# Four 32-column tiles against one full product in a bias MLP, and folded weight products in the self-attention after it

## The chip, the cores and the metric

The kernel runs on one core of one Trainium2 chip. The metric is device time in microseconds of one execution. The profile is one execution taken by the hardware profiler; its times are in microseconds from the first instruction.

## What is computed

Two layers follow each other on an input x of 2 x 512 x 32 x 32, all in fp32.

The first is a deformable attention block with 8 groups of 64 channels. Its costly part is a small network that gives a bias to every pair of a query position (1024) and a sampled key position (64), in each of 16 groups (2 images, 8 heads). Cut to what matters:

```python
pos = grid_q[:, :, None, :] - grid_kv[:, None, :, :]        # 16 x 1024 x 64 x 2
bias = jnp.sign(pos) * jnp.log1p(jnp.abs(pos))
bias = jax.nn.relu(bias @ cpb_w1 + cpb_b1)                  # 2 -> 128
bias = jax.nn.relu(bias @ cpb_w2 + cpb_b2)                  # 128 -> 128
bias = (bias @ cpb_w3 + cpb_b3)                             # 128 -> 1
attn = jax.nn.softmax(qh @ kh^T + bias, axis=-1)
out = attn @ vh
x = x + out_w out + out_b
x = x + mlp_w2 gelu(mlp_w1 bn(x) + mlp_b1) + mlp_b2         # 512 -> 2048 -> 512
```

The second is a plain self-attention over the 1024 positions of each image, with 512 channels:

```python
q, k, v = Wq x + bq, Wk x + bk, Wv x + bv
attn = softmax(q^T k / sqrt(512))
out = x + Wp (attn v) + bp
```

## The kernel before

The program is written in Tile, which places the waits and allots the buffers, and may move instructions of one engine past each other where no dependence forbids it. Four stages follow each other.

**Head.** q of all groups, the sampling offsets, the sampled keys and values. The key positions' features (`fea`) are written to a DRAM tensor `fdr` and read back in chunks, broadcast to all partitions (`st_tables`, L286).

**Bias loop.** 16 groups, each of 64 keys by 1024 queries. The x half of the first bias layer depends on the key and the query's column alone, the y half on the key and the query's row alone, so ScalarE makes a table `ta` (L292) and GpSimd a table `tb` (L295) for a chunk of 16 keys. `st_layer1` then forms one key's 128 channels x 1024 queries with one custom VectorE instruction that adds the two tables and clamps at zero (L306, tile `h1`, 6 buffers).

`st_layer2` takes a pair of keys. The 128 output channels are cut into two halves z. For each z a PSUM tile `ps2` gets 64 channels of the first key in partitions 0 to 63 and the same 64 channels of the second key in partitions 64 to 127, from four column tiles of 32 columns (L327), for each half h of the queries. ScalarE applies Relu with the bias (L333 for z = 0, `rx`) and, for z = 1, with a scale that is the third layer's weight taken positive (L336, `ry`). `st_pair` then lets VectorE add both halves, weighted, in one instruction (L342): the result still needs a sum over 64 partitions only, with signs.

`st_layer3` takes two pairs, 4 keys: one matmul of 32 columns for each pair and query half, into four column tiles of the group's score tile `sim` (L366). The weights are a window of the tile `w3s`, which is zero except in two columns, so the sums of one call land in the right rows. For the first two of a group's 16 calls (`DIRECT`) VectorE makes no sum and both halves go through matmuls. At a group's first call the product of q and k starts the accumulation (L353).

After a group's last call `softmax_steps` runs in four parts, one per loop turn: bias, transposes `pt` (L380), maximum, exponential, sum and scaling; transposes `pb` (L395); then for each half of the queries the product with the values `pa` (L402) and its copy. The loop runs over pairs; layer one is written two pairs ahead of layer two:

```python
if p + 2 < 2 * NS:
    st_layer1(p + 2)
if p < 2 * NS:
    st_layer2(p)
if 1 <= p <= 2 * NS:
    st_pair(p - 1)
if p % 2 == 1 and p >= 3:
    st_layer3(p // 2 - 1)
```

**MLP.** Output projection `pso` (L452), first product `psh` (L468), second product `psm` (L476), all full 128x128x512 matmuls; VectorE adds the residual into `xs` (L480).

**Self-attention.** The four weights are loaded into `wl_s`. For each image: q and k by `psp` (L505) with their biases on ScalarE (L509); the transposed values by `psv` (L514) with bv added on VectorE (L518); scores `pss` for 8 blocks of 128 queries (L525), softmax, transposes `psx` (L544); attention times values `psa` (L567), copied to `os_` (L571); the output projection `psf` (L575), bias and residual (L580), and the store.

Of the kernel before, what the change touches and what calls it, by code (L numbers as in the profile page):

```python
# [20 lines left out]
NSL = 16  # L21
KT = 16
DIRECT = 2
# [10 lines left out]
    ("bq", 4), ("bk", 4), ("bp", 4), ("dwb", 1), ("cb1", 1), ("cb3", 1),  # L34
    ("w1x", 1), ("w1y", 1), ("cb2a", 1), ("cb2b", 1), ("w3a", 1), ("w3b", 1), ("dww", 36),
# [10 lines left out]
def conv_seq_kernel(ctx: ExitStack, tc: tile.TileContext, x, kst, cst, vec, wsm, outw, w1, w2, wl, bv, out):  # L46
# [25 lines left out]


    sc = cp.tile([P, 4], F32, name="sc")
    nc.vector.tensor_scalar(sc[:, 0:1], col("w3b"), 0.0, 2.0, ALU.is_ge, ALU.mult)
    nc.vector.tensor_scalar(sc[:, 0:1], sc[:, 0:1], 1.0, None, ALU.subtract)
    nc.vector.tensor_tensor(sc[:, 1:2], sc[:, 0:1], col("w3b"), ALU.mult)
    nc.vector.tensor_tensor(sc[:, 2:3], sc[:, 0:1], col("w3a"), ALU.mult)
    nc.vector.tensor_tensor(sc[:, 3:4], sc[:, 1:2], col("cb2b"), ALU.mult)
    w3s = cp.tile([P, 62], F32, name="w3s")  # L80
    w3d = cp.tile([P, 62], F32, name="w3d")
    for t, src in ((w3s, sc[:, 0:1]), (w3d, col("w3a"))):
        nc.gpsimd.memset(t, 0.0)
        for u in range(2):
            nc.gpsimd.tensor_copy(t[64 * u : 64 * u + 64, 30 + u : 31 + u], src[64 * u : 64 * u + 64, :])

    dp = ctx.enter_context(tc.tile_pool(name="dp", bufs=1, space=bass.MemoryType.DRAM))
    fdr = dp.tile([NG, 4, 2 * W, KT], F32, name="fdr")
# [13 lines left out]
    with tc.tile_pool(name="ph", bufs=1) as ph, tc.tile_pool(name="ph2", bufs=2) as ph2, tc.tile_pool(  # L102
# [105 lines left out]
        for e in range(2):  # L208
            nc.vector.tensor_copy(
                kv.rearrange("p k b (e i t) -> p (k b) e i t", e=2, t=2)[:, :, e],  # L210
                pk.rearrange("p (g i e t) -> p g i e t", i=NSL, e=2, t=2)[:, :, :, e],
            )
# [45 lines left out]
        for c in range(4):  # L258
            nc.sync.dma_start(
                out=fdr[:, c, :, :].rearrange("g p j -> p g j"),  # L260
                in_=fea[0:64].rearrange("p f g (c j) -> p (f g) c j", c=4)[:, :, c, :],
            )
# [11 lines left out]
    with tc.tile_pool(name="lp", bufs=2) as lp, tc.tile_pool(  # L274
# [4 lines left out]
        NS = NG * NSL  # L279
        tabs, h1s, rxs, us, sims = {}, {}, {}, {}, {}  # L280


        def st_tables(c):
            b, k, f = groups[c // 4]
            fb = lp.tile([P, 2, W, KT], F32, name="fb", bufs=1)
            nc.sync.dma_start(  # L286
                out=fb.rearrange("p a x j -> p (a x j)"),
                in_=fdr[f * 8 + b * NCH + k, c % 4].rearrange("p j -> (p j)").partition_broadcast(P),
            )
            ta = lp.tile([P, KT, W], F32, name="ta", bufs=2)  # L290
            tb = lp.tile([P, KT, H], F32, name="tb", bufs=2)
            nc.scalar.activation(  # L292
                ta.rearrange("p j x -> p x j"), fb[:, 0], AF.Identity, bias=col("cb1"), scale=col("w1x")
            )
            nc.gpsimd.tensor_scalar(  # L295
                tb.rearrange("p j y -> p y j"), fb[:, 1], col("w1y"), 0.0, ALU.mult, ALU.add
            )
            tabs[c] = (ta, tb)

        def st_layer1(pair):  # L300
            for t in range(2):
                key = 2 * pair + t
                ta, tb = tabs[key // KT]
                j = key % KT
                h1 = lp.tile([P, HW], F32, name="h1", bufs=6)
# [7 lines left out]
                h1s[pair, t] = h1  # L313

        def paired(pair):
            return pair // 2 % NSL >= DIRECT

        def st_layer2(pair):  # L320
            h1 = [h1s.pop((pair, t)) for t in range(2)]
            for z in range(2):
                ps = zp.tile([P, 2, 512], F32, name="ps2")
                for h in range(2):
                    for q in range(4):
                        c0 = 64 * z + 32 * (q % 2)
                        nc.tensor.matmul(  # L327
                            ps[32 * q : 32 * q + 32, h, :], cw2[:, c0 : c0 + 32],
                            h1[q // 2][:, h * 512 : (h + 1) * 512], start=True, stop=True,
                        )  # L330
                if z == 0:
                    rx = lp.tile([P, 2, 512], F32, name="rx", bufs=3)
                    nc.scalar.activation(rx, ps, AF.Relu, bias=col("cb2a"))  # L333
                else:
                    ry = lp.tile([P, 2, 512], F32, name="ry", bufs=5)
                    nc.scalar.activation(ry, ps, AF.Relu, bias=sc[:, 3:4], scale=sc[:, 1:2])  # L336
            rxs[pair], us[pair] = rx, ry

        def st_pair(pair):
            if paired(pair):  # L340
                rx, ry = rxs.pop(pair), us[pair]
                nc.vector.scalar_tensor_tensor(  # L342
                    ry.rearrange("p h n -> p (h n)"), rx.rearrange("p h n -> p (h n)"), sc[:, 2:3],
                    ry.rearrange("p h n -> p (h n)"), ALU.mult, ALU.add,
                )

        def st_layer3(s):
            gi, i = divmod(s, NSL)
            b, k, f = groups[gi]
            if i == 0:  # L350
# [8 lines left out]
            for direct in (True, False):  # L359
                if direct and paired(2 * s):  # L360
                    continue
                for h in range(2):
                    for e in range(2):
                        q = 64 * h + 32 * e
                        src = rxs.pop(2 * s + e) if direct and h == 1 else (rxs if direct else us)[2 * s + e]
                        nc.tensor.matmul(  # L366
                            sims[gi][q : q + 32, :], (w3d if direct else w3s)[:, 30 - 2 * i : 62 - 2 * i],
                            src[:, h, :], start=False, stop=(not direct and i == NSL - 1),
                        )
            for e in range(2):  # L370
                us.pop(2 * s + e)

        def softmax_steps(gi):
            b, k, f = groups[gi]
            sim = sims.pop(gi)
            ss = lp.tile([P, 512], F32, name="ss", bufs=1)
# [7 lines left out]
            ex = lp.tile([P, 8, J], F32, name="ex", bufs=1)  # L384
# [11 lines left out]
            at = lp.tile([P, 512], F32, name="at", bufs=1)  # L396
# [13 lines left out]
        st_tables(0)  # L410
        st_layer1(0)
        st_layer1(1)
        for p in range(2 * NS + 2):
            if p % 8 == 1 and p // 8 + 1 < 4 * NG:
                st_tables(p // 8 + 1)
            if p + 2 < 2 * NS:
                st_layer1(p + 2)
            if p < 2 * NS:
                st_layer2(p)
            if 1 <= p <= 2 * NS:  # L420
                st_pair(p - 1)
            if p % 2 == 1 and p >= 3:
                s = p // 2 - 1
                st_layer3(s)
                if s % NSL == NSL - 1:
                    tail = softmax_steps(s // NSL)
                    due = p
            if tail is not None and p >= due:
                tail = tail if next(tail, 0) is None else None
                due = p + 1  # L430
# [55 lines left out]
    bvb = cp.tile([P, C], F32, name="bvb")  # L486
    nc.gpsimd.dma_start(out=bvb, in_=bv.partition_broadcast(P))
# [5 lines left out]
    with tc.tile_pool(name="sp", bufs=1) as sp, tc.tile_pool(  # L493
        name="sps", bufs=2, space=PSUM
    ) as sps, tc.tile_pool(name="spm", bufs=4, space=PSUM) as spm:
        for b in range(B):
            qs = sp.tile([P, NCH, HW], F32, name="qs")
            ks = sp.tile([P, NCH, HW], F32, name="ks")
            for i, (dst, bn) in enumerate(((qs, "bq"), (ks, "bk"))):
                for o in range(NCH):  # L500
                    for h in range(2):
                        n = slice(h * 512, (h + 1) * 512)
                        ps = spm.tile([P, 512], F32, tag="ps", name="psp")
                        for k in range(NCH):
                            nc.tensor.matmul(  # L505
                                ps, wl_s[:, i, k, o * P : (o + 1) * P], xs[:, k, b, n],
                                start=(k == 0), stop=(k == NCH - 1),
                            )
                        nc.scalar.activation(dst[:, o, n], ps, AF.Identity, bias=col(bn, o))  # L509
            vt = sp.tile([P, 8, C], F32, name="vt")  # L510
            for m in range(8):
                ps = spm.tile([P, 512], F32, tag="ps", name="psv")
                for k in range(NCH):
                    nc.tensor.matmul(  # L514
                        ps, xs[:, k, b, m * P : (m + 1) * P], wl_s[:, 2, k, :],
                        start=(k == 0), stop=(k == NCH - 1),
                    )
                nc.vector.tensor_tensor(vt[:, m, :], ps, bvb, ALU.add)  # L518
            aT = sp.tile([P, 8, HW], F32, name="aT")

            def scores(t):
                ps = sps.tile([P, 2, 512], F32, name="pss")
                for h in range(2):
                    for k in range(NCH):
                        nc.tensor.matmul(  # L525
                            ps[:, h, :], qs[:, k, t * P : (t + 1) * P], ks[:, k, h * 512 : (h + 1) * 512],
# [33 lines left out]

            os_ = sp.tile([P, NCH, HW], F32, tag="qs", name="os_")
            for h in range(2):
                n = slice(h * 512, (h + 1) * 512)
                for o in range(NCH):
# [6 lines left out]
                    nc.scalar.copy(os_[:, o, n], ps)  # L571
                for o in range(NCH):
# [100 lines left out]
```

## Time and profile before

| | us |
|---|---|
| median of 3 runs | 3253.16 (3252.32 to 3254.32) |
| the profiled execution | 3253.16, its span 3251.4, granted clock 0.991 |
| head, to the first layer-two product | 166 |
| bias loop, 166 to 2286 | 2120, TensorE busy 2112.1, VectorE 1823.0, ScalarE 1279.7 |
| MLP, 2286 to 2783 | 497, TensorE busy 496.2 |
| self-attention, 2783 to the end | 468, TensorE busy 457.5 |

The profile names an instruction by its line, engine and the tiles it writes and reads. "PE" is TensorE's matmuls and "PEld" its weight loads, which can lie under matmuls. The durations of single matmul records overlap and their ends are modelled; the pace is read from start to start. An fp32 matmul of the program is two records. "128*32" after a matmul is the size of the array's tile, "128x512" the moving operand.

### The profile page before, as it was taken

Reading aid. Unit: us, or ns where it says so; the run is one execution under the profiler, and the core shown is the slowest. Engines: PE = TensorE matmul, PEld = TensorE weight load, DVE = VectorE, ACT = ScalarE, POOL = GpSimd, SP = SyncE. Lnnn points to the kernel's source line nnn. Section 1 sums busy time; section 2 is a strip of 40 time slices with the busy share of each in tenths; the row PEclk is TensorE's granted clock in tenths of the full one; section 3 lists DMA queues with packets and bytes.
Section 4 is the critical chain, followed back from the end, with each engine's and each line's share of the span. In section 5 each row is a group of like instructions: output and inputs, shape, how many; then the busy total and the mean of one; then the engine's idle time right before and its main releaser. Section 6 shows DMA issues by size and latency. Waiting matters only on the chain.

```text
span 3251.4 us, 48875 instructions
## 1 busy us (share of the span) xinstructions
PE 3180.6 (98%) x21756; PEld 1138.4 (35%) x21756; DVE 2000.6 (62%) x1865; ACT 1415.4 (44%) x1329; POOL 137.8 (4%) x79
## 2 busy tenths in 40 slices
PE   8599999999999999999999999999999999999999
PEld 2344323223223232232322322322444444444444
DVE  3588989889888898898988988988010010030030
ACT  1366666656556565565665655655101101110110
POOL 0010000000000000000000000000000000000000
PEclk9799999999999999999999999999999999999999
DMA  1100000000000000000000000000200010000000
GB/s 69 36 27 20 14 14 21 14 21 14 21 14 21 14 21 14 21 14 19 15 19 16 18 17 14 21 14 1 91 1 0 0 45 8 0 0 16 10 0 26
DMA packets 21106, 60.36 MB, mean 19 GB/s; under 512 B 5984, under 2 KB 6240, under 8 KB 19744
## 3 DMA queue, kind: packets, MB, share of 16 engines
q1 hardware_dynamic: 20240, 55.84, 4.8%
q8 instruction: 171, 2.80, 0.4%
q10 hardware_dynamic: 576, 1.14, 0.1%
q0 software_dynamic: 80, 0.26, 0.0%
q14 instruction: 39, 0.32, 0.0%
HBM read 52.78 MB, written 4.46 MB: 18 GB/s over the span
## 4 chain that ended last, share of the span: by engine, by line
PE 97%; DVE 1%; ACT 1%; DMA 1%; issue 0%; SPq 0%; ACTq 0%; DVEq 0%
PE ps L327 55%; PE sim L366 8%; PE psm L476 7%; PE psh L468 7%; PE psa L567 3%; PE psp L505 3%; PE pss L525 3%; PE pc L152 2%; PE pso L452 2%; PE psf L575 2%; PE psv L514 2%; PE pa L402 1%; PE sim L353 1%; PE psq L126 0%; PE pkv L201 0%; PE psx L544 0%
## 5 line engine op out<-in xcount | busy, mean ns | idle before, releaser
L327 PE MATMUL ps<-h,kp 128*32 128x512 f32 x16384 | 1834.3, 593 | 11.7 <-DVE h L306 11.7
L306 DVE CUSTOM_DVE_ANT_1 h<-ta,tb 128x1024 f32<-128x1024 f32 x1024 | 1245.1, 1254 | 288.7 <-PE ps L327 261.5
L327 PEld LDWEIGHTS ps<-h,kp 128*32 128x32 f32 x16384 | 557.7, 110 | 1221.8 <-issue 1171.5
L333 ACT ACTIVATE rx<-ps,vs 128x1024 f32<-128x1024 f32 x512 | 571.4, 1116 | 510.9 <-PE ps L327 474.7
L336 ACT ACTIVATE ry<-ps,sc 128x1024 f32<-128x1024 f32 x512 | 614.9, 1201 | 294.2 <-PE ps L327 292.7
L342 DVE SCALAR_TENSOR_TENSOR ry<-rx,sc,ry 128x1024 f32<-128x1024 f32 x448 | 571.8, 1276 | 6.3 <-ACT ry L336 6.3
L366 PE MATMUL sim<-ry,w3s 128*32 128x512 f32 x2048 | 276.3, 592 | 0.9 <-DVE ry L342 0.9
L480 DVE SCALAR_TENSOR_TENSOR xs<-psm,vs,xs 128x512 f32<-128x512 f32 x16 | 12.0, 751 | 425.1 <-PE psm L476 425.1
L295 POOL TENSOR_SCALAR tb<-fb,vs 128x512 f32<-128x512 f32 x64 | 134.6, 2103 | 2061.0 <-DVE h L306 1899.8
L476 PE MATMUL psm<-hm,w_s 128*128 128x512 f32 x512 | 220.4, 592 | 0.0
L472 ACT ACTIVATE hm<-psh,vs 128x512 f32<-128x512 f32 x64 | 44.0, 687 | 377.7 <-PE psh L468 377.7
L468 PE MATMUL psh<-xn,w1b 128*128 128x512 f32 x384 | 165.5, 592 | 0.0
L476 PEld LDWEIGHTS psm<-hm,w_s 128*128 128x128 f32 x512 | 97.3, 190 | 122.5 <-issue 122.5
L366 PEld LDWEIGHTS sim<-ry,w3s 128*32 128x32 f32 x2048 | 69.7, 110 | 152.0 <-issue 148.9
L567 PE MATMUL psa<-aT,vt 128*128 128x512 f32 x256 | 113.9, 607 | 0.0
L525 PE MATMUL pss<-ks,qs 128*128 128x512 f32 x256 | 112.2, 592 | 0.0
L505 PE MATMUL psp<-xs,wl_s 128*128 128x512 f32 x256 | 110.3, 592 | 0.8 <-DVE xs L480 0.8
L580 DVE SCALAR_TENSOR_TENSOR res<-psf,vs,xs 128x512 f32<-128x512 f32 x16 | 12.0, 752 | 156.0 <-PE psf L575 156.0
L518 DVE TENSOR_TENSOR vt<-psv,bvb 128x512 f32<-128x512 f32 x16 | 11.1, 691 | 154.7 <-PE psv L514 154.7
L468 PEld LDWEIGHTS psh<-xn,w1b 128*128 128x128 f32 x384 | 73.0, 190 | 91.8 <-issue 91.8
L292 ACT ACTIVATE ta<-fb,vs 128x512 f32<-128x512 f32 x64 | 84.1, 1315 | 42.5 <-DMA fb<-fdr 32.9
L535 ACT ACTIVATE ex<-pss,mx 128x1024 f32<-128x1024 f32 x16 | 17.8, 1114 | 124.6 <-DVE mx L532 124.6
(114 smaller groups left out, 1148.7 us busy)
## 6 DMA issues: line engine op xcount, KB each, us to landing
fb<-fdr SPq DMA_DIRECT2D x64, 512.0 KB, 3.6
xs<-in_x SPq DMA_DIRECT2D x8, 512.0 KB, 9.7
w_s<-in_w SPq DMA_DIRECT2D x4, 1024.0 KB, 13.6
wl_s<-in_wl SPq DMA_DIRECT2D x4, 1024.0 KB, 7.8
out<-res SPq DMA_DIRECT2D x16, 256.0 KB, 2.0
w1b<-in_w SPq DMA_DIRECT2D x3, 1024.0 KB, 7.2
ow_s<-in_outw SPq DMA_DIRECT2D x1, 1024.0 KB, 6.2
w1a<-in_w SPq DMA_DIRECT2D x1, 1024.0 KB, 8.5
```

The lines of the kernel that those rows point to most:

```text
L295: nc.gpsimd.tensor_scalar(tb.rearrange("p j y -> p y j"), fb[:, 1], col("w1y"), 0.0, ALU.mult, ALU.add)
L306: nc.vector._custom_dve(TENSOR_ADD_SAT, out=h1.rearrange("p (y x) -> p y x", x=W), in0=ta[:, j, :].unsqueeze(1).to_broadcast([P, H, W]), i ...
L327: nc.tensor.matmul(ps[32 * q : 32 * q + 32, h, :], cw2[:, c0 : c0 + 32], h1[q // 2][:, h * 512 : (h + 1) * 512], start=True, stop=True,)
L333: nc.scalar.activation(rx, ps, AF.Relu, bias=col("cb2a"))
L336: nc.scalar.activation(ry, ps, AF.Relu, bias=sc[:, 3:4], scale=sc[:, 1:2])
L342: nc.vector.scalar_tensor_tensor(ry.rearrange("p h n -> p (h n)"), rx.rearrange("p h n -> p (h n)"), sc[:, 2:3], ry.rearrange("p h n -> p ...
L366: nc.tensor.matmul(sims[gi][q : q + 32, :], (w3d if direct else w3s)[:, 30 - 2 * i : 62 - 2 * i], src[:, h, :], start=False, stop=(not dir ...
L468: nc.tensor.matmul(ps, w1i, xn2[:, k, :], start=(k == 0), stop=(k == NCH - 1),)
L476: nc.tensor.matmul(ps, w2_s[:, i, o * P : (o + 1) * P], hm[:, i, :], start=(i == 0), stop=(i == NF - 1),)
L505: nc.tensor.matmul(ps, wl_s[:, i, k, o * P : (o + 1) * P], xs[:, k, b, n], start=(k == 0), stop=(k == NCH - 1),)
L525: nc.tensor.matmul(ps[:, h, :], qs[:, k, t * P : (t + 1) * P], ks[:, k, h * 512 : (h + 1) * 512], start=(k == 0), stop=(k == NCH - 1),)
L567: nc.tensor.matmul(ps, vt[:, m, o * P : (o + 1) * P], aT[:, m, n], start=(m == 0), stop=(m == 7),)
```

## The change

The change has two parts and belongs to two stages. Constants, tables and layouts follow: the kernel has one table chunk of 32 keys where it had two of 16, the key order of a group is laid out anew, the third layer's weights stand in one column of `w3p`, and `bv` goes into the packed vectors.

*Bias loop.* Layer two is one full 128x128 product for a key and query half, with all 128 channels of one key in the 128 partitions. VectorE's sum and the direct case are gone. Layer three takes a step of 2 keys with 128 channels each, so 512 steps in all. The loop runs over steps; layer one is written one step ahead; layer three of two steps is written together, at every second step.

```diff
-        def st_layer1(pair):
-            for t in range(2):
-                key = 2 * pair + t
-                ta, tb = tabs[key // KT]
-                j = key % KT
-                h1 = lp.tile([P, HW], F32, name="h1", bufs=6)
+        def st_layer1(s):
+            ta, tb = tabs[s // 16]
+            for e in range(2):
+                j = 2 * (s % 16) + e
+                h1 = lp.tile([P, HW], F32, name="h1", bufs=4)
...
-        def st_layer2(pair):
-            h1 = [h1s.pop((pair, t)) for t in range(2)]
-            for z in range(2):
+        def st_layer2(s):
+            for e in range(2):
+                h1 = h1s.pop((s, e))
                 ps = zp.tile([P, 2, 512], F32, name="ps2")
                 for h in range(2):
-                    for q in range(4):
-                        c0 = 64 * z + 32 * (q % 2)
-                        nc.tensor.matmul(
-                            ps[32 * q : 32 * q + 32, h, :], cw2[:, c0 : c0 + 32],
-                            h1[q // 2][:, h * 512 : (h + 1) * 512], start=True, stop=True,
-                        )
-                if z == 0:
-                    rx = lp.tile([P, 2, 512], F32, name="rx", bufs=3)
-                    nc.scalar.activation(rx, ps, AF.Relu, bias=col("cb2a"))
-                else:
-                    ry = lp.tile([P, 2, 512], F32, name="ry", bufs=5)
-                    nc.scalar.activation(ry, ps, AF.Relu, bias=sc[:, 3:4], scale=sc[:, 1:2])
-            rxs[pair], us[pair] = rx, ry
-
-        def st_pair(pair):
-            if paired(pair):
-                rx, ry = rxs.pop(pair), us[pair]
-                nc.vector.scalar_tensor_tensor(
-                    ry.rearrange("p h n -> p (h n)"), rx.rearrange("p h n -> p (h n)"), sc[:, 2:3],
-                    ry.rearrange("p h n -> p (h n)"), ALU.mult, ALU.add,
-                )
+                    nc.tensor.matmul(
+                        ps[:, h, :], cw2, h1[:, h * 512 : (h + 1) * 512], start=True, stop=True
+                    )
+                h2 = lp.tile([P, 2, 512], F32, name="h2", bufs=6)
+                nc.scalar.activation(h2, ps, AF.Relu, bias=col("cb2"))
+                h2s[s, e] = h2
...
-            for direct in (True, False):
-                if direct and paired(2 * s):
-                    continue
-                for h in range(2):
-                    for e in range(2):
-                        q = 64 * h + 32 * e
-                        src = rxs.pop(2 * s + e) if direct and h == 1 else (rxs if direct else us)[2 * s + e]
-                        nc.tensor.matmul(
-                            sims[gi][q : q + 32, :], (w3d if direct else w3s)[:, 30 - 2 * i : 62 - 2 * i],
-                            src[:, h, :], start=False, stop=(not direct and i == NSL - 1),
-                        )
+            h2 = [h2s.pop((s, e)) for e in range(2)]
+            for h in range(2):
+                for e in range(2):
+                    q = 64 * h + 32 * e
+                    nc.tensor.matmul(
+                        sims[gi][q : q + 32, :], w3p[:, R - 1 - r : 2 * R - 1 - r], h2[e][:, h, :],
+                        start=False, stop=(r == R - 1),
+                    )
...
         st_tables(0)
+        st_tables(1)
         st_layer1(0)
...
+        for s in range(NS + 2):
+            if s % 16 == 2 and s // 16 >= 1 and s // 16 + 1 < 2 * NG:
+                st_tables(s // 16 + 1)
+            if s + 1 < NS:
+                st_layer1(s + 1)
+            if s < NS:
+                st_layer2(s)
+            if s % 2 == 0 and s >= 2:
+                st_layer3(s - 2)
+                st_layer3(s - 1)
+                if s % R == 0:
+                    tail = softmax_steps(s // R - 1)
+                    due = s
+            if tail is not None and s >= due:
                 tail = tail if next(tail, 0) is None else None
-                due = p + 1
+                due = s + 2
```

*Self-attention.* The products Wq'Wk and WpWv of the weights are formed once (`gw`), and the vectors Wk'bq and Wp bv + bp (`ub`). Then q is projected with Wq'Wk and multiplied with x itself for the scores, which leaves out terms that are the same for all keys of a query; the values are projected with WpWv, so that attention times values is already the output.

```diff
+        gw = sp.tile([P, 2, NCH, C], F32, name="gw")
+        ub = sp.tile([P, 2, NCH], F32, name="ub")
+        for i in range(2):
+            for k in range(NCH):
+                ps = spm.tile([P, 512], F32, tag="ps", name="psg")
+                for o in range(NCH):
+                    nc.tensor.matmul(
+                        ps, wl_s[:, 2 * i, o, k * P : (k + 1) * P], wl_s[:, 2 * i + 1, o, :],
+                        start=(o == 0), stop=(o == NCH - 1),
+                    )
+                nc.scalar.copy(gw[:, i, k, :], ps)
+        for i, bn in enumerate(("bq", "bv")):
+            for k in range(NCH):
+                ps = spm.tile([P, 512], F32, tag="ps", name="psu")
+                for o in range(NCH):
+                    nc.tensor.matmul(
+                        ps[:, 0:1], wl_s[:, 2 * i + 1, o, k * P : (k + 1) * P], col(bn, o),
+                        start=(o == 0), stop=(o == NCH - 1),
+                    )
+                if i == 0:
+                    nc.vector.tensor_copy(ub[:, i, k : k + 1], ps[:, 0:1])
+                else:
+                    nc.vector.tensor_tensor(ub[:, i, k : k + 1], ps[:, 0:1], col("bp", k), ALU.add)
...
-            for i, (dst, bn) in enumerate(((qs, "bq"), (ks, "bk"))):
...
-                nc.vector.tensor_tensor(vt[:, m, :], ps, bvb, ALU.add)
+                nc.vector.tensor_copy(vt[:, m, :], ps)
...
-                            ps[:, h, :], qs[:, k, t * P : (t + 1) * P], ks[:, k, h * 512 : (h + 1) * 512],
+                            ps[:, h, :], qs[:, k, t * P : (t + 1) * P], xs[:, k, b, h * 512 : (h + 1) * 512],
...
-                    nc.scalar.copy(os_[:, o, n], ps)
-                for o in range(NCH):
-                    ps = spm.tile([P, 512], F32, tag="ps", name="psf")
-                    for k in range(NCH):
-                        nc.tensor.matmul(
-                            ps, wl_s[:, 3, k, o * P : (o + 1) * P], os_[:, k, n],
-                            start=(k == 0), stop=(k == NCH - 1),
-                        )
                     res = sp.tile([P, 512], F32, name="res", bufs=3)
                     nc.vector.scalar_tensor_tensor(
-                        res, ps, col("bp", o), xs[:, o, b, n], ALU.add, ALU.add
+                        res, ps, ub[:, 1, o : o + 1], xs[:, o, b, n], ALU.add, ALU.add
                     )
```

## The prediction

> **What bounds the kernel now.** I read the page first (busy shares, then the chain that ended last), then the groups by line, then the chain in order of time, and last a timeline of one group boundary.
>
> ```profile
> span 3251.4 us, 48875 instructions
> ...
> PE 3180.6 (98%) x21756; PEld 1138.4 (35%) x21756; DVE 2000.6 (62%) x1865; ACT 1415.4 (44%) x1329; POOL 137.8 (4%) x79
> ...
> PE 97%; DVE 1%; ACT 1%; DMA 1%; issue 0%; SPq 0%; ACTq 0%; DVEq 0%
> ```
>
> TensorE carries 97% of the chain; no other engine ends a wait worth a per cent. So only TensorE time counts, unless an edit starves TensorE. Groups by line (count | busy us, mean ns | idle before):
>
> ```profile
> L327 PE MATMUL ps<-h,kp 128*32 128x512 f32 x16384 | 1834.3, 593 | 11.7 <-DVE h L306 11.7
> L306 DVE CUSTOM_DVE_ANT_1 h<-ta,tb 128x1024 f32<-128x1024 f32 x1024 | 1245.1, 1254 | 288.7 <-PE ps L327 261.5 <-POOL tb L295 16.6 <-ACT ta L292 10.6
> L342 DVE SCALAR_TENSOR_TENSOR ry<-rx,sc,ry 128x1024 f32<-128x1024 f32 x448 | 571.8, 1276 | 6.3 <-ACT ry L336 6.3
> L366 PE MATMUL sim<-ry,w3s 128*32 128x512 f32 x2048 | 276.3, 592 | 0.9 <-DVE ry L342 0.9
> L366 PE MATMUL sim<-rx,w3d 128*32 128x512 f32 x256 | 34.8, 598 | 0.0
> ```
>
> The reader is to see the counts: 16384 records for 8192 written matmuls, so each fp32 matmul is two records. L306 waits for TensorE, not the reverse (11.7 us of idle before L327, all at the start). The chain in order of time (start, us, what) gives the true pace, which the 593 ns of a record, overlapped, does not:
>
> ```profile
> 866.80 6.87 PE ps L327 x64
> 874.53 6.87 PE ps L327 x64
> ...
> 2356.40 54.93 PE psm L476 x128
> ...
> 2782.98 55.20 PE psp L505 x128
> ...
> 2960.41 13.73 PE psf L575 x32
> ```
>
> I call a **set** one full 128x128x512 matmul (2 records), or four 32-column matmuls side by side (8 records). Full: 54.93 / 64 = 0.858 us. Column tiles: 64 records are 8 sets, 6.87 / 8 = 0.859 us. The same price. From one line of L327 to the next, 874.53 - 866.80 = 7.73 us = 9 sets: 8 of layer two, 1 of layer three, no gap.
>
> Now the price of changing the array's tiling (timeline, TensorE's rows at a group boundary):
>
> ```profile
> 967.86 1.07 PE L353 MATMUL sim<-qpad,ksb 64*64 64x512 f32 x2
> 968.86 0.66 PE L395 MATMUL pb<-kp,ex 128*128 128x128 f32 x4
> 969.44 1.07 PE L353 MATMUL sim<-qpad,ksb 64*64 64x512 f32 x2
> 970.44 1.07 PE L366 MATMUL sim<-rx,w3d 128*32 128x512 f32 x8
> 971.33 1.04 PE L366 MATMUL sim<-ry,w3s 128*32 128x512 f32 x8
> 972.30 1.07 PE L402 MATMUL pa<-at,vsb 64*64 64x512 f32 x2
> 973.30 3.64 PE L327 MATMUL ps<-h,kp 128*32 128x512 f32 x32
> ```
>
> Start to start, a set between two changes takes 1.00 us instead of 0.858; the set after entering 128*32 takes 0.89 (+0.03, its first weights exposed), the set before leaving it 0.97 (+0.11). And with 128x128 weights the first load is dearer (weight loads at the start of the last stage; the first two passes are 0.53 apart, the later ones 0.43, so +0.10):
>
> ```profile
> 2782.98 0.30 PEld L505 LDWEIGHTS psp<-xs,wl_s 128*128 128x128 f32 x2 [1.67 <-DVE xs L480]
> 2783.51 0.19 PEld L505 LDWEIGHTS psp<-xs,wl_s 128*128 128x128 f32 x1 [0.24 <-issue]
> 2783.94 0.19 PEld L505 LDWEIGHTS psp<-xs,wl_s 128*128 128x128 f32 x1 [0.24 <-issue]
> ```
>
> **What the Trainium skill says.** "TensorEngine Tiling (Array Packing)", Tiling Modes: changing the tiling mode, not just the tile, drains TensorE. The trace agrees: 0.11 us at each change above, none between tiles of one mode. "TensorE: Matmul & The Clock Gate", LDWEIGHTS: a load costs its columns / 1.2 ns, so 128 columns 107 ns and 32 columns 27 ns. The trace shows +0.10 and +0.03 where a load is exposed, which agrees. "FP8 and Floating Point Precision", TensorE Precision Notes: true fp32 is four passes whatever the tiling; the equal 0.858 and 0.859 agree.
>
> **The change part by part**, against the profiled execution (3251.4 us; the median of the runs is 1.8 above it).
>
> (a) Layer two: 2 keys were 2 x 2 x 4 column tiles, 4 sets; they become 4 full matmuls, 4 sets. 2048 sets either way: 0. Fewer weight loads (4096 records for 16384), but loads lay under matmuls already.
>
> (b) Layer three: VectorE no longer sums two channel halves, so each step of 2 keys needs a set of its own. Before, 256 sets and 32 more for the direct steps, 288 (2048 + 256 records / 8). After, 512. +224 x 0.8585 = **+192.3 us**, all on TensorE.
>
> (c) Tiling changes: before, layers two and three were both 128*32. After, layer two is 128*128, and layer three comes in pairs of steps, so once in two steps the array goes 128*128 to 128*32 and back: 256 visits. Going out 0.09 (969.44 minus the last of four transposes, 0.109 apart, leaves 0.20 where 0.109 is usual) + 0.03 = 0.12; coming back 0.11 drain + 0.10 weights = 0.21. 256 x 0.33 = **+84.5**. No change 128*32 to 128*128 for fp32 products stands in the trace: below, if the first load hides and the drain is paid once, 0.12 (31 us); above 0.45 (115 us). I take 0.33, from its measured pieces.
>
> (d) Group boundary: pb recurs 131.87 us apart (836.99, 968.86); 146 sets are 125.3, so a boundary is 6.5 us. After: transposes pt and pb lie in layer two's own mode, 0.44 each; the two sim products come next to each other in other columns, 0.86 + 0.16; pa twice 1.02: 3.9 to 4.0. 16 x -2.6 = **-41** (down to 0 if the order splits them as now).
>
> (e) VectorE loses L342's 448 x 1.276 us and gives nothing back, since TensorE hid it. ScalarE has 1024 Relus of about 1.12 us (L333), 1143 against 1186: hidden. But layer one now runs one step of 4.3 us ahead with 4 buffers, where it ran 2 pairs ahead with 6. A softmax puts some 3.7 us of VectorE work, with waits inside, in its queue, and layer two waits behind it: **+8**, half a microsecond a group (0 to 40).
>
> (f) Start: the first table is twice as large (1024 KB per load), its ta about 1.3 us longer, and ta(1) stands in ScalarE's queue ahead of Relu: **+3** (0 to 8). Later tables are loaded 14 steps ahead and stay hidden.
>
> (g) Last stage. The key projection is 64 of L505's 128 products, and psf is 64: -128 sets. Forming the two weight products adds 32: net -96 x 0.8585 = **-82.4**. The two bias vectors add 32 one-column products, 64 records paced by their weights; psx, 8 records in 0.87 us, gives 0.109: **+7**. The 0.8 us wait for xs at 2782 is covered by the new weight products: **-0.8**. The copies os, the addition of bv and its broadcast DMA go from engines that were waiting: 0. Scores with xs for ks and the value product keep count and shape.
>
> Sum: 192.3 + 84.5 - 41 + 8 + 3 - 82.4 + 7 - 0.8 = +170.6. 3251.4 + 170.6 = 3422.0; with the 1.8 to the median, **3424 us**.
>
> **The rivals.**
>
> *Cheap switching.* Column tiles of full row height may share the array with full products better than the 64-row tiles do. Then 0.12 a visit: 3424 - 54 = 3370. For it: entering 128*32 cost only 0.03 beyond the drain. Against: L395 to L353 paid at both sides.
>
> *More changes, or starving.* If the order of execution separates the two steps of layer three (the trace shows pt placed inside a layer-two set and pb between the two sim products, so the written order isn't kept), visits double: +84, 3508. A starved layer two, 2 us a group, gives 3424 + 24 = 3448. For it: lead cut to one step. Against: VectorE falls from 110.6 busy of 127 us in the loop to about 58%.
>
> *Faster.* One mechanism: a full product in layer two streams faster than four column tiles, since a quarter of the weight loads is left. It decides only if it saves 171 us over 1024 keys, 0.167 of 1.717 us: passes 0.387 apart for 0.429. At 0.375 the kernel would take 3424 - 4 x 0.054 x 1024 = 3203. Against: psm and pss already run full products with a load each, at exactly 0.429.
>
> **How the numbers follow.** Forecast 0.70, more changes 0.15, cheap switching 0.10, faster 0.04, no change 0.01 (several errors cancelling). The forecast's own bounds are 3370 to 3490 ((c) -54 to +31, (d) up to +41, (e) -8 to +32, not all at once); with the upper rival I say 3370 to 3500. Under 0.2% (6.5 us) nothing can be told from no change. Faster 0.04, same 0.01, slower 0.95.
>
> **What would show it.** Layer two in runs of 16 records lasting about 6.9 us, and layer three of 16 in about 1.9; L366's counterpart with 4096 records; about 8.9 us from one visit to the next; boundaries of 4 us; the last stage about 76 us shorter with no L575. Wrong if TensorE shows idle released by VectorE in the loop, if visits are 512, or if two visits lie under 8.7 us apart.

## The result, and the profile after

| | before | after |
|---|---|---|
| median, us | 3253.47 (4 runs) | 3417.32 (4 runs, 3415.55 to 3419.95) |
| span of the profiled execution | 3251.4 | 3415.3 |
| head, to the first layer-two product | 165.9 | 166.2 |
| bias loop | 2119.7 | 2356.3 |
| MLP | 497.4 | 498.1 |
| self-attention | 468.4 | 394.7 |

The ratio is 1.0505 (95% interval 1.0486 to 1.0523): slower, 164 us more, where 171 more were forecast. The stages are cut at the first `ps`, `pso` and `psp` (after: `psg`) product. Every profiled execution of this document has a mean granted clock of 0.989 to 0.991.

The page of after, its head, its busy line and its chain by engine:

```profile
span 3415.3 us, 28243 instructions
...
PE 3346.8 (98%) x11132; PEld 1339.9 (39%) x11132; DVE 1535.5 (45%) x1419; ACT 1353.1 (40%) x1273; POOL 75.7 (2%) x42
...
PE 98%; DVE 1%; ACT 1%; DMA 0%; issue 0%; ACTq 0%; SPq 0%; DVEq 0%
```

There are twenty thousand instructions fewer and VectorE is 465 us less busy, and yet the time is 164 us longer: TensorE was 97% of the chain before and is 98% now. The loop's groups in after, by line:

```profile
L304 PE MATMUL ps<-h,kp 128*128 128x512 f32 x4096 | 1828.6, 599 | 12.5 <-DVE h L290 12.5
L290 DVE CUSTOM_DVE_ANT_1 h<-ta,tb 128x1024 f32<-128x1024 f32 x1024 | 1295.5, 1268 | 955.2 <-PE ps L304 943.8 <-ACT ta L277 11.3
L327 PE MATMUL sim<-h,w3p 128*32 128x512 f32 x4096 | 493.0, 598 | 0.0
```

Layer three's products (now L327) have 4096 records where they had 2304, in groups of eight to a set. Layer one now waits 943.8 us for TensorE where it waited 261.5: the time taken from VectorE became idle time of VectorE. The only wait of layer two for layer one, 12.5 us, is the start, as before.

The chain of after in order of time, over one group boundary (start, us, what):

```profile
716.87 1.85 PE sim L327 x16
718.72 7.06 PE ps L304 x16
725.78 1.85 PE sim L327 x16
727.64 7.07 PE ps L304 x16
...
754.39 1.91 PE ps L304 x4
756.31 0.44 PE pt L339 x4
756.75 5.15 PE ps L304 x12
761.90 1.01 PE sim L317 x4
762.90 1.85 PE sim L327 x16
```

Two steps recur after 725.78 - 716.87 = 8.91 us; over the five periods from 707.95 to 752.54 it is 8.92. Ten sets are 8.585 us: 1.72 for layer three and 6.87 for layer two. The two rows stand 0.14 and 0.20 us above these; the sum, 0.335 us, is the price of one visit to layer three. At the boundary pt costs 0.44 and both sim products 1.01, as forecast. The four records of pb fall between a visit and layer two and take 0.59, but the layer two behind them is then back at 6.87, so the pair costs what was forecast.

The last stage of after, at its start (windows; us, busy of each engine, granted clock, DMA):

```profile
3048.00:3053.00 5.00, 5.00 (x46) 4.85 (x44) 0.79 (x5) 0.58 (x1) 0.00 (x0) 1.00 0.00 0
3053.00:3058.00 5.00, 5.00 (x24) 4.48 (x24) 0.47 (x3) 0.00 (x0) 0.00 (x0) 0.54 0.02 3
3058.00:3062.00 4.00, 4.00 (x8) 1.66 (x7) 0.00 (x0) 0.00 (x0) 0.00 (x0) 0.72 0.00 0
```

While the one-column products psu run (3048 to 3057), the granted clock falls to half after some 5 us: there are 46 TensorE records in the first window and 24 in the next, at a mean clock of 0.54. The first wide products after them still run at a lowered clock, 0.72 over 3058 to 3062.

### The profile page after: what moved, and what is told of

Same layout as the page of the kernel before. It is cut to its first block, busy times and chain, and to the rows that moved or that the text cites. A ratio compares the mean times of both kernels' runs of the same rounds, so it can differ in the third digit from the quotient of the medians.

```text
span 3415.3 us, 28243 instructions
## 1 busy us (share of the span) xinstructions
PE 3346.8 (98%) x11132; PEld 1339.9 (39%) x11132; DVE 1535.5 (45%) x1419; ACT 1353.1 (40%) x1273; POOL 75.7 (2%) x42
## 4 chain that ended last, share of the span: by engine, by line
PE 98%; DVE 1%; ACT 1%; DMA 0%; issue 0%; ACTq 0%; SPq 0%; DVEq 0%
PE ps L304 53%; PE sim L327 14%; PE psm L433 6%; PE psh L425 6%; PE psa L544 3%; PE pss L504 3%; PE pc L139 2%; PE pso L409 2%; PE psp L484 2%; PE psv L493 2%; PE pa L361 1%; PE psg L460 1%; PE pkv L188 0%; PE psq L113 0%; PE sim L317 0%; PE psx L523 0%
## 5 line engine op out<-in xcount | busy, mean ns | idle before, releaser
L304 PE MATMUL ps<-h,kp 128*128 128x512 f32 x4096 | 1828.6, 599 | 12.5 <-DVE h L290 12.5
L290 DVE CUSTOM_DVE_ANT_1 h<-ta,tb 128x1024 f32<-128x1024 f32 x1024 | 1295.5, 1268 | 955.2 <-PE ps L304 943.8
L308 ACT ACTIVATE h<-ps,vs 128x1024 f32<-128x1024 f32 x1024 | 1136.1, 1113 | 1056.4 <-PE ps L304 1055.2
L304 PEld LDWEIGHTS ps<-h,kp 128*128 128x128 f32 x4096 | 756.6, 190 | 1064.6 <-issue 1050.3
L327 PE MATMUL sim<-h,w3p 128*32 128x512 f32 x4096 | 493.0, 598 | 0.0
L327 PEld LDWEIGHTS sim<-h,w3p 128*32 128x32 f32 x4096 | 107.2, 109 | 348.4 <-issue 348.1
L280 POOL TENSOR_SCALAR tb<-fb,vs 128x1024 f32<-128x1024 f32 x32 | 73.7, 2302 | 2276.8 <-DVE h L290 2115.0
L504 PE MATMUL pss<-xs,qs 128*128 128x512 f32 x256 | 112.2, 592 | 0.0
L277 ACT ACTIVATE ta<-fb,vs 128x1024 f32<-128x1024 f32 x32 | 77.5, 2421 | 36.5 <-DMA fb<-fdr 33.9
L139 PE MATMUL pc<-qpad,dg 128*128 128x512 f32 x72 | 66.0, 1093 | 0.0
L409 PE MATMUL pso<-att,ow_s 128*128 128x512 f32 x128 | 58.3, 615 | 0.7 <-ACT att L365 0.7
```

What stands on the lines that cost most here:

```text
L139: nc.tensor.matmul(pc.rearrange("p (g y x) -> p g y x", y=8, x=8), dg, qpad[:, :, ky : ky + 29 : 4, kx : kx + 29 : 4], start=(t == 0), sto ...
L277: nc.scalar.activation(ta.rearrange("p j x -> p x j"), fb[:, 0], AF.Identity, bias=col("cb1"), scale=col("w1x"))
L290: nc.vector._custom_dve(TENSOR_ADD_SAT, out=h1.rearrange("p (y x) -> p y x", x=W), in0=ta[:, j, :].unsqueeze(1).to_broadcast([P, H, W]), i ...
L304: nc.tensor.matmul(ps[:, h, :], cw2, h1[:, h * 512 : (h + 1) * 512], start=True, stop=True)
L308: nc.scalar.activation(h2, ps, AF.Relu, bias=col("cb2"))
L327: nc.tensor.matmul(sims[gi][q : q + 32, :], w3p[:, R - 1 - r : 2 * R - 1 - r], h2[e][:, h, :], start=False, stop=(r == R - 1),)
```

## The experiments

The theory is that the two parts act on separate stages and add up, and that the loop has 224 more sets and 256 visits at a price of changing the array's tiling, less a cheaper group boundary. The rivals are that the parts interact, or that the 0.335 us a visit is a wait for ScalarE or VectorE, not the array.

**The fold alone** (loop of before, last stage of after; the edit against before is the self-attention part of the change, of which this is the start).

```diff
-    bvb = cp.tile([P, C], F32, name="bvb")
...
+        gw = sp.tile([P, 2, NCH, C], F32, name="gw")
+        ub = sp.tile([P, 2, NCH], F32, name="ub")
```

> The bias loop of before with the self-attention of after. My theory (the two parts act on separate stages and add up): the last stage is 394.7 us as in after, against 468.4, and the whole 3253.5 - 73.7 = 3180 us. Rival (the fold's gain depends on the new loop, for instance through the clock or through memory that the loop's smaller tables free): anything above 3190.

3180.5 us, ratio 0.9776 (0.9759 to 0.9792). The loop took 2119.7 us, as before. The last stage took 397.4 us, not the expected 394.7; the total came within a microsecond of 3180 because the head was 1.5 us shorter than before, as heads vary (164.6 to 166.2 over after and the five kernels below that change only its loop). Of the 2.7 us in the last stage, 1.7 lie at the bias vectors (the last section shows the lines) and, on balance, 1.1 behind the two waits for the softmax. Behind the first of these waits the same instructions ran at full clock in after and at half here (windows as above, first after, then the fold alone):

```profile
3178.00:3181.00 3.00, 2.75 (x13) 1.82 (x14) 1.39 (x3) 0.00 (x0) 0.00 (x0) 1.00 0.00 0
```

```profile
2940.00:2943.00 3.00, 2.41 (x9) 2.10 (x10) 1.57 (x3) 0.00 (x0) 0.00 (x0) 0.50 0.00 0
```

**The new loop alone** (last stage of before; the edit against after takes the fold out again).

```diff
-        gw = sp.tile([P, 2, NCH, C], F32, name="gw")
...
+            for i, (dst, bn) in enumerate(((qs, "bq"), (ks, "bk"))):
```

> The bias loop of after with the self-attention of before. My theory: 3417.3 + 73.7 = 3491 us, the loop 2356 us as in after. Rival (parts interact): off by more than 5 us, or the sum of the two single effects differs from +163.9 by more than 5 us.

3490.8 us, one run; loop 2356.3. The single effects, -73.3 and +237.0, sum to +163.8; both together gave +163.85. That they agree to a tenth is luck: over all runs of this document the head took 164.3 to 168.0 us, and the same last stage 394.6 to 397.7. Within these 3 to 4 us the parts don't interact, and the loop, where it would matter, took the same time with either last stage.

**Layer two in column tiles of 32, all else as after.**

```diff
-                    nc.tensor.matmul(
-                        ps[:, h, :], cw2, h1[:, h * 512 : (h + 1) * 512], start=True, stop=True
-                    )
+                    for q in range(0, P, 32):
+                        nc.tensor.matmul(
+                            ps[q : q + 32, h, :], cw2[:, q : q + 32],
+                            h1[:, h * 512 : (h + 1) * 512], start=True, stop=True,
+                        )
```

> After, with layer two's full product written as four column tiles of 32, so that layers two and three have one tiling and the array doesn't change between them; products, VectorE, ScalarE and buffers are as in after. My theory (0.335 us a visit is the change of tiling): two steps take 8.585 us instead of 8.92, the loop loses 256 x 0.335 = 86 us and gets back 1.2 to 2.7 us at each of 16 boundaries, since the transposes now change the tiling: 3350 to 3375 us. Rival (the 0.335 us is a wait for ScalarE's Relu or for VectorE's h, which stays): two steps stay at 8.92 us and the time at 3417 or a little above.

3347.9 us, ratio to before 1.0290 (1.0275 to 1.0305). Its chain in order of time:

```profile
781.87 6.87 PE ps L305 x64
788.74 1.72 PE sim L329 x16
790.45 6.87 PE ps L305 x64
797.32 1.72 PE sim L329 x16
```

Two steps take 8.58 us: the 0.335 us a visit is gone with the tiling change, with ScalarE and VectorE doing just what they did. A group takes 142.3 us against 146.5; its boundary rose from 3.8 to 4.9 us, a little less than expected. This settles the rival of a wait in the steps.

**A visit after every step.**

```diff
-            if s % 2 == 0 and s >= 2:
-                st_layer3(s - 2)
+            if 1 <= s <= NS:
                 st_layer3(s - 1)
```

> After, with layer three written after every step instead of for two steps at every second one: 512 visits for 256, the same products. My theory: one step takes 4.29 + 0.335 = 4.63 us, +256 x 0.335 = 86 us, 3503 us. Rival (the 0.335 us is a wait that depends on data, not on visits): within 10 us of 3417.

3504.8 us, one run; TensorE's timeline (start, us, engine, line, records):

```profile
743.22 3.70 PE L304 MATMUL ps<-h,kp 128*128 128x512 f32 x8
746.85 1.06 PE L327 MATMUL sim<-h,w3p 128*32 128x512 f32 x8
747.85 3.70 PE L304 MATMUL ps<-h,kp 128*128 128x512 f32 x8
```

A step takes 747.85 - 743.22 = 4.63 us, as expected, and the loop 85.9 us more than in after: the price goes with the visit.

**A visit for four steps.**

```diff
-            if s % 2 == 0 and s >= 2:
-                st_layer3(s - 2)
-                st_layer3(s - 1)
+            if s % 4 == 0 and s >= 4:
+                for d in range(4):
+                    st_layer3(s - 4 + d)
```

with `h2` at 9 buffers and `ss`, `ex`, `at` at one.

> After, with layer three written for four steps at every fourth: 128 visits for 256; h2 has 9 buffers for 6, and ss, ex and at one each for two, which makes room. My theory: four steps take 17.17 + 0.34 = 17.5 us for 17.84, -128 x 0.335 = -43 us, 3374 us. Rival (longer visits starve ScalarE's buffers, so that TensorE waits for Relu): less gained than 30 us, and idle TensorE time released by ScalarE in the loop.

3378.3 us, one run; the loop was 39.6 us shorter, not 43. Four steps take 799.60 - 782.10 = 17.50 us as expected, without idle time (chain in order of time, over a group boundary):

```profile
762.40 1.00 PE pa L361 x2
763.40 7.06 PE ps L304 x16
770.46 1.00 PE pa L361 x2
771.46 7.06 PE ps L304 x16
778.52 3.57 PE sim L327 x32
782.10 13.93 PE ps L304 x32
796.03 3.57 PE sim L327 x32
799.60 10.50 PE ps L304 x24
```

The rest was given back at the boundary. In after both `pa` products lay between a visit and layer two; here the second lies inside layer two, which pays another 0.2 us to come back from it (7.06 for 6.87).

**A quarter of layer three left out.**

```diff
-            for h in range(2):
+            for h in range(2) if r % 4 != 1 else ():
```

> After, with the layer-three products of every fourth step left out (128 of 512 steps, so a part of the bias is missing from the scores); each visit stays, with one step or two in it. My theory (a step's four products are one set on TensorE): -128 x 0.858 = -110 us, 3307 us, a visit of one step 0.858 us shorter than one of two. Rival (the four products don't run wholly side by side, or part of a visit is fixed): a saving off from 110 by more than 5 us.

3309.2 us, one run; the loop was 109.4 us shorter, 0.855 us for each step left out. From start to start, visits of one step take 1.00 us, of two 1.86 (timeline of TensorE):

```profile
771.79 1.07 PE L327 MATMUL sim<-h,w3p 128*32 128x512 f32 x8
772.79 7.13 PE L304 MATMUL ps<-h,kp 128*128 128x512 f32 x16
779.85 1.93 PE L327 MATMUL sim<-h,w3p 128*32 128x512 f32 x16
781.71 7.13 PE L304 MATMUL ps<-h,kp 128*128 128x512 f32 x16
```

So 224 sets are worth about 191.5 us.

**Layer two in column tiles of 64.** As with tiles of 32, with `q : q + 64`.

> After, with layer two's full product written as two column tiles of 64. The tiling still changes twice a visit. My theory (a change costs a drain of about 0.1 us and then the first weights, by their columns): entering layer two saves the load of 64 columns, 0.05 us a visit, so two steps take about 8.87 us, the loop 14 us less, 3404 us. Rival (only full 128x128 products cost, tiles share the array): as with tiles of 32, 8.585 us and about 3348. Rival (the price is the same for any change): 8.92 and 3417.

3426.1 us (ratio 1.0532, 1.0516 to 1.0547): a miss in the total. TensorE's timeline:

```profile
718.60 7.09 PE L305 MATMUL ps<-h,kp 128*64 128x512 f32 x32
725.62 1.93 PE L329 MATMUL sim<-h,w3p 128*32 128x512 f32 x16
727.47 7.09 PE L305 MATMUL ps<-h,kp 128*64 128x512 f32 x32
```

Two steps take 727.47 - 718.60 = 8.87 us, which was expected: the price falls by 0.05 us where the weights that come first fall from 128 columns to 64. What I left out was the boundary: the transposes pt and pb, which had layer two's tiling in after, now change it and pt splits a set, so a group takes 147.1 us against 146.5, and the loop 7.9 us more.

**Both kept, with two orders changed.** Loop of before, folded attention, and, against the fold alone:

```diff
             nc.vector.tensor_scalar(ss, sim, col("cb3"), None, ALU.add)
+            yield
             pt = mip.tile([P, 512], F32, tag="mi", name="pt")
...
             yield
+            yield
             exf = ex.rearrange("p a j -> p (a j)")
...
-        for i in range(2):
+        for i, bn in enumerate(("bq", "bv")):
...
                 nc.scalar.copy(gw[:, i, k, :], ps)
-        for i, bn in enumerate(("bq", "bv")):
-            for k in range(NCH):
                 ps = spm.tile([P, 512], F32, tag="ps", name="psu")
```

> The bias loop of before and the self-attention of after, with two orders changed: at a group's end one more turn of the loop lies between ss and pt and one more before pb, so that pt doesn't split a set of layer two and pb not the two sim products; and each bias vector's products stand between the weight products. My theory: 3180.5, less 0.86 (pt) and about 1.0 (sim) at 16 boundaries, -29, less 3.5 us for the clock in the last stage: 3148 us. Rival (the softmax, now later, delays the copies of att or the next group's sim, or VectorE is too full in this loop to take it): 3175 or more.

3152.2 us, ratio 0.9689 (0.9673 to 0.9706). The loop is 24.7 us shorter than before, not 29. A group takes 130.18 us for 131.87, which is 27 us over 16 groups; the other 2.3 us came back outside the equal group periods. Both splits are gone, and the sim products run side by side:

```profile
820.43 3.62 PE L327 MATMUL ps<-h,kp 128*32 128x512 f32 x32
823.98 0.66 PE L381 MATMUL pt<-kp,ss 128*128 128x128 f32 x4
824.57 3.64 PE L327 MATMUL ps<-h,kp 128*32 128x512 f32 x32
828.14 1.08 PE L353 MATMUL sim<-qpad,ksb 64*64 64x512 f32 x4
```

The last stage took 393.1 us, without a fall of the clock while the bias vectors are formed. From the first `psg` to the end of the first image's `psp` it took 62.3 us, for 67.3 in the fold alone and 65.7 in after:

```profile
2757.00:2792.00 35.00, 34.16 (x124) 18.86 (x124) 1.86 (x8) 4.24 (x8) 0.00 (x0) 1.00 0.00 0
```

**More sums on VectorE.** On top of that, `DIRECT` from 2 to 1 and to 0.

```diff
-DIRECT = 2
+DIRECT = 1
```

> The kernel with both parts kept (loop of before, folded attention, the two orders changed), with one direct step a group instead of two: VectorE sums 32 pairs more, TensorE has 16 sets fewer. My theory (TensorE alone bounds the loop while VectorE has room): -16 x 0.858 = -14 us, 3138 us; VectorE 41 us busier. Rival (VectorE, in bursts at a group's end, is already too late): above 3148.

```diff
-DIRECT = 2
+DIRECT = 0
```

> The same with no direct step: VectorE sums all 512 pairs, some 2015 us of work in a loop of 2068. My theory: -27 us if VectorE keeps up, 3125 us; but the direct steps lie where the softmax's VectorE work lies, so part of it comes back as TensorE waiting for VectorE: 3125 to 3150. Rival (VectorE becomes the bound): above 3152.

3139.9 us (ratio 0.9650, 0.9636 to 0.9664) and 3126.2 us (0.9607, 0.9591 to 0.9623): they gained 12.3 and 26.0 us, against 14 and 27 expected. VectorE is busy 1902 of 2069 us in the last one's loop, TensorE 2061:

```profile
166.00:2235.00 2069.00, 2061.12 (x18686) 645.40 (x18683) 1902.22 (x1647) 1277.21 (x1136) 136.59 (x63) 1.00 0.05 17
```

VectorE at 92% still ends no wait of TensorE that before didn't have, so none of the waiting came that I had thought likely; its work in the loop was also less than the 2015 us I had put down. This version is 127 us faster than before and 291 faster than after.

## Why the prediction was right

The forecast was +170.6 us on the profiled execution; it became +163.9. Its mechanism held, more sets on TensorE and a price for each change of tiling. That the sum came so near is partly luck, since terms of some 13 us that came out lower stand against some 6 us that came out higher. By its steps:

- (a) Layer two, 0: right. Without the change of tiling, eight sets take 6.87 us in either form.
- (b) Layer three, +192.3: right; leaving steps out gives 0.855 us a set, +191.5.
- (c) Tiling, 256 x 0.33 = +84.5: right, 0.335, +85.8. The price was put together from a 64*64 change, an entry into 128*32 and an exposed weight load, none of them the change in question; each way came within 0.02 us (0.14 for 0.12, 0.20 for 0.21), nearer than its own limits of 31 to 115 us let one expect. The 0.53 us of its weight loads lie between the first load and the third, since the first row holds two; the 0.10 us beyond the usual 0.43 stands. The tiles of 64 support the parts: half the exposed columns, 0.05 us less. The split into a drain and a load was not tried by itself. "TensorEngine Tiling (Array Packing)", Tiling Modes, says that a change drains the array; same tiling, no gap, is what the tiles of 32 show.
- (d) Boundary, -41: right. 131.87 - 146 sets = 6.5 us before; 146.54 - 160 sets - 16 visits = 3.8 after; 16 x -2.7 = -43.
- (e) VectorE's lead, +8: mis-sized, it measured next to nothing. Outside the start and the drain of the last group, TensorE's matmuls waited once for VectorE in the whole loop, 0.9 us before the first pb. VectorE was busy 1357 of the loop's 2356 us, and one step of lead was enough. The longest of these waits (us in total, times, longest; the 12.5 are the start, the 3.9 and the 0.9 of pt the drain):

```profile
PE ps L304 <- DVE h L290: 12.5, 1, 12.5
PE pb L354 <- DVE ex L349: 4.9, 2, 3.9
PE pt L339 <- DVE ss L336: 0.9, 1, 0.9
```

- (f) Start, +3: mis-sized, +0.3, which the spread of the heads (164.3 to 168.0) hides. On the chain the larger table cost 2.2 us (its load 4.68 for 3.48, ta 2.37 for 1.34), and two writes of `fdr` for four gave 1.4 back.
- (g) Last stage, -76.2: -73.7. The 96 sets were right. The bias vectors took 8.7 us for 7, and the wide products after them 1.7 more, since the clock fell to half. Against that, the products behind the two softmax waits came 1.7 us cheaper than in before, where the clock fell both times; in after it fell once. The wait for xs was not covered: `psg` waited 0.8 us for VectorE's last `xs`, although it reads only weights; that it waits for PSUM or memory which that instruction still holds is likely but wasn't tried.

Not in the sum: 1.9 us more outside the equal group periods, of which 0.7 lie ahead of the first pb, with the one wait, and the rest in the last group; and 0.7 at the start of the MLP, which ran a little longer at half clock.

The rival of cheap switching fell with the 0.335 us; that of more changes fell because the order of execution kept both steps of a visit together, and the kernel with visits of one step shows what it would have cost, 3504.8 us. The range to 3500 had left that out, though the prediction itself put this rival at 3508. The starved layer two fell with the waits above; and a full product streams no faster than four tiles, though it loads its weights in a quarter of the records. What that rival calls a pass is one record, two to a product and 0.429 us apart in either form. The traces show these two; that an fp32 product is four passes, as the prediction cites, no run here shows.

## What to carry to other kernels

Count the work of the engine that bounds the kernel in its own units (here sets of the array) before counting instructions: the change removed 42% of the instructions and 465 us of VectorE's time, and added 224 sets to the one engine that had no room. Work that VectorE does while TensorE is the bound is free until VectorE ends a wait; here that held up to 92% busy. Where two kinds of matmul alternate and a profile shows a price for the change, as here 0.335 us, write both with the same tiling of the array (70 us less in this loop, after what the boundaries took back), or make the visits long; and test the halves of a double change separately, since one half here was worth 73 us and the other cost 237.

## What was not expected of the hardware

I did not expect a fall of the clock inside busy TensorE time: 32 one-column products (64 records) with 128 columns of weights, back to back for 8.7 us, brought the granted clock to half, with the engine busy by the profile all along. Set among wide products, in runs of 8 records between runs of 8 wide ones, they left it at full. The cost also varies from kernel to kernel: with the fold alone, the chain shows

```profile
2808.99 9.56 PE psu L512 x64
2818.55 30.04 PE psp L527 x64
```

against 8.72 and 29.21 us in after, for the same instructions. Why it falls earlier in one kernel than in the other is open, and I didn't try how short a run of such products must be to keep the clock.
